# The additions and subtractions of five rotations, on GpSimd and not on VectorE

## The chip, the core and the metric

The kernel runs on one core of a Trainium2 chip. The metric is the device time of one execution in microseconds, as the median of repeated runs. The core has five engines with a queue each: TensorE (PE) for matrix products and transposes, VectorE (DVE), ScalarE (ACT) and GpSimd (POOL) for elementwise work, and SyncE (SP), which here only issues DMAs. GpSimd issues some DMAs too. Each engine takes its instructions in the order in which they stand in its queue.

## What is computed

Two transformer layers on x of 4 x 512 x 512 floats. Layer 0 is an attention of 32 heads of 16 with one shared key and value, and a linear layer with dequantised weights. Layer 1 is an attention of 32 query heads of 128 over 8 key and value heads, with rotary position embedding, and a feed-forward part with ternary octonion weights. Cut to the part that matters here:

```python
def _rotate_half(x):
    x1, x2 = (x[..., :HEAD_DIM // 2], x[..., HEAD_DIM // 2:])
    return jnp.concatenate([-x2, x1], axis=-1)
...
q = (hidden_states @ Wq.T).reshape(bsz, q_len, N_HEADS, HEAD_DIM).transpose(0, 2, 1, 3)
...
q = q * cos + _rotate_half(q) * sin
k = k * cos + _rotate_half(k) * sin
...
scores = jnp.einsum('bhqd,bhkd->bhqk', q, k) * scale
...
x = x + _layernorm(_L1_attn_ref(_layernorm(x, axis=-1), ...), axis=-1)
```

## The kernel before

**Numbers.** Matrix products run on a rounded float type (F32R). To keep accuracy a value is split into a high part (a cast) and a low part (value minus high part), and a product becomes three: high by high, high by low, low by high (`mm3`, lines 183 to 185; `mm3_gen`, lines 160 to 162). A 128 x 512 product over 512 is so 12 matmuls.

**Stages.** First comes layer 0 for the four batches (class `A1`, with the tail of each 128-row tile in `A2.post`: output projection, layer norms, linear layer, layer 1's first norm, and the values of layer 1, products with the weights called `wv`). `post` takes tiles through `add_norm`, whose norm has a power on GpSimd (L108), and adds a shift to a tile on GpSimd (L813) before it is stored for the last stage. Then `phase_b` does layer 1's attention, and class `C` the feed-forward part.

**Units.** `phase_b` works in 32 units, u = 0 to 31: unit u is key head g = u // 4 of batch b = u % 4, with the four query heads of that group. For each unit there is one `kproj` (the rotated key) and four `qproj` (the rotated queries q0 to q3), 12 matmuls each. In a unit's 16 steps, `score` makes one 128-row block of scores of one query head: matmuls into a PSUM bank of `ps` (L960 and L961 for the first block, with a mask addition L962 on VectorE; L965 to L967 for the others), a fused mask and row minimum on VectorE (L969), the exponential on ScalarE (L973), a reciprocal (L975) and a scaling on GpSimd (L976). `trans` transposes four of these (L985) and splits them (L988, L989), `pv` multiplies by the values (L998 to L1000) and `oproj` projects into the accumulator. The projections of unit u + 1 stand among the steps of unit u. Unit 0's projections have no unit before them: they stand where layer 0's last tiles end. This stretch, from some 640 to 700 us, is called the passage below.

**Rotation.** `rope` (lines 845 to 854) takes a projection in PSUM and makes both parts of the rotated tile: three products on VectorE (L848, L850, L851), an addition (L852) on the engine `eng`, a cast on ScalarE (L853), and a subtraction (L854) on `eng`. Its scratch tiles `rp_a` and `rp_b` come from a pool with one buffer each, so a rotation can start only when the one before has read `rp_a` for the last time, at L854. A PSUM bank of a projection is free after L851.

**Banks.** Unit 0's projections use the three `ps` banks that the scores use too (`proj_bank`); later ones use the two `mm` banks, shared with `oproj` and the last tiles of layer 0.

**Weights.** `load_w` loads a head's weight twice: as F32R by a DMA from GpSimd's queue (L888, `w_h`), and as it is by a DMA from SP's queue (L890, `raw`, one buffer), and subtracts on GpSimd (L891, `w_l`). SP also issues the copies of `Tern.expand` (L1145) and the loads of the input tiles (L898, L899).

**Order.** The program is recorded in the order of the Python code, and a scheduler then sets the order of the instructions in every queue from its own model of when each could run. A change of one instruction's engine can so move others, in every queue.

Of the kernel before, what the change touches and what calls it, by code (L numbers as in the profile page):

```python
# [42 lines left out]
def f(ap):  # L43
    return ap.bitcast(F32)
# [134 lines left out]
def mm3(nc, ps, lh, ll, rh, rl, ks):  # L179

    n = len(ks)
    for j, k in enumerate(ks):
        nc.tensor.matmul(ps, lh(k), rh(k), start=(j == 0), stop=False)  # L183
        nc.tensor.matmul(ps, lh(k), rl(k), start=False, stop=False)  # L184
        nc.tensor.matmul(ps, ll(k), rh(k), start=False, stop=(j == n - 1))  # L185
# [659 lines left out]
def rope(nc, tmp, dst_h, dst_l, ps, cos, sin, eng):  # L845

    a = tmp.tile([128, S], F32, name="rp_a", tag="rp_a")
    nc.vector.tensor_tensor(a, ps, cos, ALU.mult)  # L848
    r = tmp.tile([128, S], F32, name="rp_b", tag="rp_b")
    nc.vector.tensor_tensor(r[0:64], ps[64:128], sin[0:64], ALU.mult)  # L850
    nc.vector.tensor_tensor(r[64:128], ps[0:64], sin[64:128], ALU.mult)  # L851
    eng.tensor_tensor(a, a, r, ALU.add)  # L852
    nc.scalar.copy(dst_h, a)  # L853
    eng.tensor_tensor(dst_l, a, f(dst_h), ALU.subtract)  # L854


def phase_b(tc, nc, c, aps, xt_d, wk_d, v_d, acc, xp, P, tern, tail):

    if True:
        tmp = P(name="bt", bufs=1)  # L860
# [59 lines left out]
        def proj_bank(u):  # L920

            if u == 0:
                return psS.tile([128, S], F32, name="ps", tag="ps")
            return mmp.tile([128, S], F32, name="mm", tag="mm")

        def kproj(u):
            wh, wl = W["k", u // 4]
            xh, xl = X[u]
            ps = proj_bank(u)
            mm3(nc, ps, lambda k: wh[:, bass.ts(k, 128)], lambda k: wl[:, bass.ts(k, 128)],  # L930
                lambda k: xh[:, k], lambda k: xl[:, k], range(KC))
            k = kvp.tile([128, 2, S], F32R, name="k", tag="k")
            rope(nc, tmp, k[:, 0], k[:, 1], ps, cosk, sink, nc.vector if u < 1 else nc.gpsimd)
            K[u] = k

        def qproj(u, j):
            h = 4 * (u // 4) + j
            wh, wl = W["q", h]
            xh, xl = X[u]
            ps = proj_bank(u)  # L940
            mm3(nc, ps, lambda k: wh[:, bass.ts(k, 128)], lambda k: wl[:, bass.ts(k, 128)],
                lambda k: xh[:, k], lambda k: xl[:, k], range(KC))
            qh = qp.tile([128, S], F32R, name="qh", tag="qh")
            ql = qp.tile([128, S], F32R, name="ql", tag="ql")
            rope(nc, tmp, qh, ql, ps, cosq, sinq, nc.vector if u < 1 else nc.gpsimd)
            Q[u, j] = qh, ql

        PS = {}
# [76 lines left out]
        cosk, sink, cosq, sinq = (cp.tile([128, S], F32, name=n) for n in ("cosk", "sink", "cosq", "sinq"))  # L1025
# [4 lines left out]
        for j in range(4):  # L1030
            wh, wl = (wqp.tile([128, 512], F32R, name="w_" + e, tag="w_" + e) for e in "hl")
            split(nc, wh, wl, first[:, j], nc.gpsimd)
            W["q", j] = wh, wl
        kproj(0)
        for j in range(4):
            qproj(0, j)
# [7 lines left out]
        for p in range(NU * 16 + 12):  # L1044
            G, j = p // 4, p % 4
            u, qb = G // 4, G % 4
# [16 lines left out]
            if j == 1 and u + 1 < NU:  # L1063
                qproj(u + 1, qb)
                if (u + 1) % 4 == 3 and u // 4 < 7:
                    load_w("q", u // 4 + 1, qb)
            if j == 3 and qb == 0 and u + 1 < NU:
                kproj(u + 1)
                if (u + 1) % 4 == 3 and u // 4 < 7:
                    load_wk(u // 4 + 1)  # L1070
# [333 lines left out]
```

## Time and profile before

| | us |
|---|---|
| median of 3 runs (2329.95 to 2330.2) | 2330.18 |
| the profiled execution's own time | 2329.53 |
| span of the profiled execution, first to last instruction | 2327.8 |
| TensorE busy | 2276.1 |
| VectorE busy | 1578.9 |
| ScalarE busy | 1069.9 |
| GpSimd busy | 1174.8 |

In the profile's lines, `out<-in` are tile names, L numbers are lines of the kernel, `x` is a count, and `[t <-E tile L]` is the idle time of the engine before the instruction and what ended it. The waits view lists who waited for whom: total us, times, longest. "PEclk" is the share of TensorE's full clock that was granted. The time of the execution is 1.7 us more than its span.

### The profile page before, as it was taken

The numbers are of one execution on the slowest core, as the hardware profiler recorded it, in microseconds if no ns is written. First come the engines' busy times: TensorE is split into PE (matmuls) and PEld (weight loads), VectorE is DVE, ScalarE is ACT, GpSimd is POOL, SyncE is SP. The second block draws the span as 40 slices with busy tenths as digits, with TensorE's granted clock in tenths as the row PEclk, the third lists the DMA queues.
The fourth block names the chain that finished last, engine by engine and source line by source line (L and its number), as shares of the span: only waits on it lengthen the run. The fifth ranks groups of instructions, "written<-read, shape, count | busy, mean of one in ns | idle before, by whom it ended". The sixth has DMA issues, their size and how long they took to land.

```text
span 2327.8 us, 35950 instructions
## 1 busy us (share of the span) xinstructions
PE 2276.1 (98%) x11638; PEld 1789.9 (77%) x11638; DVE 1578.9 (68%) x4662; ACT 1069.9 (46%) x2408; POOL 1174.8 (50%) x1388
## 2 busy tenths in 40 slices
PE   7999999999989999999999999999999999999998
PEld 5666566666678888888888888888888888878886
DVE  6766767685477777777777777777777778764443
ACT  6655545454334444444444444444444445543332
POOL 3323443434246665765665765765665767522211
PEclk9999999999999999999999999999999999999999
DMA  3655463525362413413313313323322312051000
GB/s 92 200 156 176 116 164 74 160 82 163 123 212 82 127 66 98 125 66 101 122 66 104 119 66 106 117 66 109 113 67 106 98 63 78 10 158 37 32 23 19
DMA packets 155535, 236.31 MB, mean 102 GB/s; under 512 B 26274, under 2 KB 91042, under 8 KB 146516
## 3 DMA queue, kind: packets, MB, share of 16 engines
q1 hardware_dynamic: 137732, 195.33, 26.9%
q0 software_dynamic: 14768, 35.92, 5.4%
q10 hardware_dynamic: 2848, 2.76, 0.4%
q8 instruction: 93, 1.52, 0.3%
q14 instruction: 94, 0.77, 0.1%
HBM read 180.03 MB, written 61.83 MB: 104 GB/s over the span
## 4 chain that ended last, share of the span: by engine, by line
PE 87%; issue 4%; DMA 4%; DVE 2%; ACT 2%; POOL 1%; SPq 0%; ACTq 0%; POOLq 0%; DVEq 0%
PE mm L183 11%; PE mm L184 11%; PE mm L185 11%; PE pt L985 6%; PE mm L160 3%; PE mm L161 3%; PE mm L162 3%; PE po L998 3%; PE po L999 3%; PE po L512 3%; PE po L1000 3%; PE ps L965 3%; PE ps L966 3%; PE ps L967 3%; PE gu L1218 3%
## 5 line engine op out<-in xcount | busy, mean ns | idle before, releaser
L976 POOL TENSOR_TENSOR s<-s,r 128x384 f32<-128x384 f32 (+3 forms) x512 | 359.0, 720 | 117.5 <-DVE r L975 106.8
L973 ACT ACTIVATE s<-s,mn 128x384 f32<-128x384 f32 (+3 forms) x512 | 286.1, 560 | 239.8 <-DVE mn L969 230.6
L852 POOL TENSOR_TENSOR rp_a<-rp_a,rp_b 128x512 f32<-128x512 f32 x155 | 200.2, 1292 | 279.8 <-DVE rp_b L851 266.7
L988 ACT CAST ph<-pt 128x512 fp32r<-128x512 f32 x320 | 181.4, 586 | 289.9 <-PE pt L985 287.6
L461 DVE CUSTOM_DVE_ANT_0 jk<-ps,mask 128x384 bf16<-128x384 f32 (+3 forms) x512 | 228.8, 482 | 73.1 <-PE ps L457 72.0
L989 DVE TENSOR_TENSOR pl<-pt,ph 128x512 fp32r<-128x512 f32 x320 | 216.3, 687 | 39.8 <-ACT ph L988 36.6
L969 DVE CUSTOM_DVE_ANT_0 s<-ps,mask 128x384 f32<-128x384 f32 (+2 forms) x384 | 203.2, 552 | 39.2 <-PE ps L967 18.9
L499 ACT ACTIVATE pe<-pt 128x512 f32<-128x512 f32 x307 | 175.1, 601 | 90.8 <-PE pt L496 82.2
L985 PE MATMUL pt<-ident,s 128*128 128x128 f32 x1280 | 211.8, 272 | 0.2 <-DVE pl L989 0.2
L183 PE MATMUL mm<-w_h,oh 128*128 128x512 f32 x512 | 203.7, 398 | 0.9 <-ACT oh L1004 0.9
L184 PE MATMUL mm<-w_l,oh 128*128 128x512 f32 x512 | 201.9, 394 | 0.5 <-POOL w_l L891 0.5
L185 PE MATMUL mm<-w_h,ol 128*128 128x512 f32 x512 | 200.4, 391 | 0.0
L985 PEld LDWEIGHTS pt<-ident,s 128*128 128x128 f32 x1280 | 164.3, 140 | 45.4 <-DVE pl L989 0.4
L183 PE MATMUL mm<-xh,w_h 128*128 128x512 f32 x496 | 198.8, 401 | 0.0
L185 PE MATMUL mm<-xh,w_l 128*128 128x512 f32 x496 | 197.0, 397 | 0.0
L501 POOL TENSOR_SCALAR_AFFINE_SELECT pe<-pe 128x512 f32<-128x512 f32 x128 | 83.4, 655 | 224.4 <-ACT pe L499 219.4
L184 PE MATMUL mm<-xl,w_h 128*128 128x512 f32 x496 | 195.8, 395 | 0.0
L854 POOL TENSOR_TENSOR ql<-rp_a,qh 128x512 fp32r<-128x512 f32 x124 | 160.3, 1293 | 47.4 <-ACT qh L853 46.3
L848 DVE TENSOR_TENSOR rp_a<-mm,cosq 128x512 f32<-128x512 f32 x124 | 85.6, 690 | 120.2 <-PE mm L185 89.7
L1004 ACT CAST oh<-po 128x512 fp32r<-128x512 f32 x128 | 74.4, 582 | 152.8 <-PE po L1000 152.4
L965 PE MATMUL ps<-k,qh 128*128 128x384 f32 (+2 forms) x384 | 141.2, 368 | 1.0 <-DVE mn L969 0.9
L108 POOL TENSOR_TENSOR ln_rs<-ln_ve,mhalf 128x1 f32<-128x1 f32 x112 | 63.7, 576 | 152.8 <-DVE ln_ve L106 139.0
(349 smaller groups left out, 5853.4 us busy)
## 6 DMA issues: line engine op xcount, KB each, us to landing
xh<-xt SPq DMA_DIRECT2D x32, 1024.0 KB
xl<-xt SPq DMA_DIRECT2D x32, 1024.0 KB
raw<-in_a_wo SPq DMA_DIRECT2D x32, 256.0 KB
vh<-v SPq DMA_DIRECT2D x32, 256.0 KB
vl<-v SPq DMA_DIRECT2D x32, 256.0 KB
w_h<-in_a_wo POOLq DMA_DIRECT2D x32, 256.0 KB, 3.3
m_d<-t_d SPq DMA_DIRECT2D x192, 42.5 KB
raw<-in_a_wq SPq DMA_DIRECT2D x28, 256.0 KB
```

What stands on the lines that cost most here:

```text
L183: nc.tensor.matmul(ps, lh(k), rh(k), start=(j == 0), stop=False)
L184: nc.tensor.matmul(ps, lh(k), rl(k), start=False, stop=False)
L185: nc.tensor.matmul(ps, ll(k), rh(k), start=False, stop=(j == n - 1))
L461: nc.vector.tensor_tensor_reduce(out=jk[:, :nk], in0=p, in1=self.c.mask[:, 384 - 128 * qb:512], scale=-1.0, scalar=3e38, op0=ALU.add, op1= ...
L852: eng.tensor_tensor(a, a, r, ALU.add)
L965: nc.tensor.matmul(ps[:, :nk], qh[:, qs], k[:, 0, :nk], start=True, stop=False)
L969: nc.vector.tensor_tensor_reduce(out=s[:, :nk], in0=ps[:, :nk], in1=mask, scale=-1.0, scalar=3e38, op0=ALU.add, op1=ALU.min, accum_out=mn)
L973: nc.scalar.activation(s[:, :nk], s[:, :nk], AF.Exp, bias=mn, scale=-1.0, accum_out=l)
L976: nc.gpsimd.tensor_tensor(s[:, :nk], s[:, :nk], r.to_broadcast([128, nk]), ALU.mult)
L985: nc.tensor.transpose(pt[:, j], PS[u, qb, j][:, bass.ts(kb, 128)], c.ident)
L988: nc.scalar.copy(ph, pt)
L989: nc.vector.tensor_tensor(pl, pt, f(ph), ALU.subtract)
```

## The change

`kproj` and `qproj` hand `rope` the engine for its addition and its subtraction. Before, this was VectorE for unit 0 and GpSimd for the 31 others; after, it is GpSimd for all.

```diff
-            rope(nc, tmp, k[:, 0], k[:, 1], ps, cosk, sink, nc.vector if u < 1 else nc.gpsimd)
+            rope(nc, tmp, k[:, 0], k[:, 1], ps, cosk, sink, nc.gpsimd)
...
-            rope(nc, tmp, qh, ql, ps, cosq, sinq, nc.vector if u < 1 else nc.gpsimd)
+            rope(nc, tmp, qh, ql, ps, cosq, sinq, nc.gpsimd)
```

Five rotations of unit 0 are concerned (one key, four queries), with two instructions each.

## The prediction

> **What bounds the kernel now.** I read the page's first part, then the busy time by stage, then TensorE's waits inside the stage of the change and after it, then the timeline there.
>
> ```profile
> PE 2276.1 (98%) x11638; PEld 1789.9 (77%) x11638; DVE 1578.9 (68%) x4662; ACT 1069.9 (46%) x2408; POOL 1174.8 (50%) x1388
> ```
>
> TensorE is busy 98% of the span, so a change counts only where it opens or closes one of TensorE's gaps. The next view cuts the span into attention of layer 0, the passage to layer 1 (unit 0's rotations lie here), the other units, and the rest; columns are length, PE, PEld, DVE, ACT, POOL busy, TensorE's clock, DMA.
>
> ```profile
> 0.00:640.00 640.00, 607.40 (x3338) 406.61 (x3338) 422.07 (x1586) 336.50 (x622) 237.00 (x356) 0.99 0.48 137
> 640.00:700.00 60.00, 53.62 (x238) 43.34 (x239) 45.47 (x110) 22.43 (x51) 29.20 (x37) 0.94 0.65 206
> 700.00:2030.00 1330.00, 1328.62 (x6772) 1110.18 (x6771) 968.53 (x2630) 606.76 (x1562) 841.13 (x918) 1.00 0.28 91
> 2030.00:2328.00 298.00, 286.44 (x1294) 229.72 (x1292) 142.86 (x337) 104.23 (x174) 67.42 (x79) 0.99 0.18 53
> ```
>
> From 700 to 2030 TensorE lacks 1.4 us of 1330: there is nothing to win. In the 60 us of the passage it lacks 6.4 us, and its clock is 0.94. TensorE's waits in that window:
>
> ```profile
> PE ps L960 <- DVE mn L969: 2.7, 1, 2.7
> PE ps L183 <- DVE rp_b L851: 2.1, 1, 2.1
> PE ps L965 <- DVE mn L969: 0.9, 2, 0.4
> PE mm L160 <- ACT ph L150: 0.7, 1, 0.7
> ```
>
> The second ends with the first rotation's last product (L851), which the change does not touch. The first is the one in reach: the fourth score of unit 0 needs a `ps` bank that the first L969 frees. Why is L969 late? VectorE's timeline, with TensorE's score below:
>
> ```profile
> 675.12 0.69 DVE L848 TENSOR_TENSOR rp_a<-mm,cosk 128x512 f32<-128x512 f32 x1 [1.21 <-POOL ql L854]
> ...
> 680.70 0.69 DVE L848 TENSOR_TENSOR rp_a<-mm,cosq 128x512 f32<-128x512 f32 x1 [1.20 <-POOL k L854]
> ...
> 686.28 0.69 DVE L848 TENSOR_TENSOR rp_a<-mm,cosq 128x512 f32<-128x512 f32 x1 [2.76 <-POOL ql L854]
> ...
> 689.01 0.28 DVE L969 CUSTOM_DVE_ANT_0 s<-ps,s 128x128 f32<-128x128 f32 x1
> ...
> 689.36 0.57 PE L960 MATMUL ps<-k,qh 128*128 128x256 f32 x1 [2.72 <-DVE mn L969]
> ```
>
> L969 stands in VectorE's queue behind the rotations. `rp_a` has one buffer, so rotations form one chain, and each L848 waits for the subtraction (L854) of the one before. Nine rotations begin before L969: five of unit 0 and four of unit 1.
>
> **The cost of an operation.** From the instructions on `rp_a`:
>
> ```profile
> L852 POOL TENSOR_TENSOR rp_a<-rp_a,rp_b x155: 1265/1292/1316, 671.0 to 2018.0; 128x512 f32<-128x512 f32 x155
> L854 POOL TENSOR_TENSOR ql<-rp_a,qh x124: 1274/1294/1308, 673.8 to 2020.7; 128x512 fp32r<-128x512 f32 x124
> L852 DVE TENSOR_TENSOR rp_a<-rp_a,rp_b x5: 682/684/691, 643.4 to 666.0; 128x512 f32<-128x512 f32 x5
> L854 DVE TENSOR_TENSOR ql<-rp_a,qh x4: 683/692/750, 653.4 to 667.4; 128x512 fp32r<-128x512 f32 x4
> ```
>
> Ten instructions leave VectorE (10 x 0.69 = 6.9 us) and come to GpSimd (10 x 1.29 = 12.9 us). One rotation's turn is 680.70 - 675.12 = 5.58 us on GpSimd; on VectorE the shortest is 663.90 - 659.47 = 4.43 us (L848 to L848). So the chain's bare price is 5 x 1.15 = 5.75 us. [...]
>
> **The order moves too.** The scheduler writes another order for all engines from the middle of the passage. Up to the fourth score TensorE gets the same amount of work in both programs (kproj and three qproj of unit 1 included); what differs is that only eight rotations, not nine, begin before the first L969, and L969 is put after the eighth's second product. One turn less is 5.58 us, which nearly pays the 5.75. So I follow the new order with the trace's durations (matmul of 512 columns 0.233 us apart, L848 to L851's end 2.10, handover to GpSimd 0.14, add 1.28, cast 0.62 with 0.04 and 0.07 beside it, subtraction 1.29, 0.04 back).
>
> k starts at 639.91 as before; its products end at 642.0, so TensorE's 2.1-us wait stays. Add 642.14, cast, subtraction to 645.44. The rotation of q0 starts at 645.5 (before: 648.22, as it stood behind the split of a transposed tile). TensorE does q3's projection at 648.2, ahead of most of the wv products. On GpSimd q0's add stands behind L813 (1.57) and three L108 (0.53 each): 648.6; its subtraction behind two more L813: 653.3 to 654.6. That delay is covered: q1's L848 stands in VectorE's queue behind two splits whose transposes TensorE reaches at 654.0 to 655.0, so q1 starts at 656.45. Then one L813 in its turn: q2 starts at 662.9. q3 stands behind the mask addition (L962) of the second score, which TensorE reaches at 669.05, behind wv products and kproj: 669.75 (GpSimd was done at 669.0). From here the chain runs free at 5.58: q(1,0) 675.3, k(1) 680.9, q(1,1) 686.5. Two products later, at 687.9, comes L969, 0.29 long: the fourth score starts at 688.2 instead of 689.36, **1.15 us earlier**. All along TensorE has matmuls: qproj(1,1) is reached at 678.0 with its bank free at 677.4, qproj(1,2) at 683.6 with its bank free at 683.0. Work ends at 686.4, so the wait shrinks from 2.7 to about 1.8 us.
>
> What else queues behind the moved instructions: the last tiles' L108 comes up to 5.6 us later (649.04 to about 654.6), but its transposes are not reached before 665.6. L813's x2 stores go out a little later on SP's queue and are read only in the last stage; VectorE's 6.9 us are returned beside an idle queue and bring nothing by themselves.
>
> After the scores: on GpSimd the six DMA issues of `w_h` (L888, 689.72 to 693.05, so 3.33 us) follow k(1)'s subtraction at 686.45, then q(1,1)'s add, one L891 and four L976 (0.36 each): 693.9, when unit 0's first transposes start; before it was 694.21. q(1,1)'s subtraction comes behind four longer L976, at 696.1 to 697.4, and holds q(1,2)'s L848 until 697.8 and so the bank of qproj(1,3) until 699.9; before, qproj(1,3) started at 701.24. That lead of 1.2 agrees with the first. At 717.34 TensorE waited 0.46 us for the fourth `w_l` (L891); its raw load is now issued before the eight L1145 copies and not behind them, and I count 0.15 of it as gained.
>
> From there TensorE is full. Whether it stays so is the one thing no row shows. I counted, in the two orders, for each TensorE wait on another engine, how much matmul work lies between its last TensorE ancestor and itself: under 1.5 us in 24 of 1836 waits before, in 9 of 1869 after; under 2.5 us in 92 and 51. The cover is no thinner, so I keep the 1.4 us lost there, with +-1 us.
>
> **The clock.** The rows first:
>
> ```profile
> 686.00:690.00 4.00, 1.28 (x6) 0.84 (x5) 3.53 (x11) 1.25 (x4) 1.73 (x3) 0.93 0.22 66
> 690.00:693.00 3.00, 3.00 (x16) 3.00 (x15) 2.65 (x16) 2.69 (x12) 3.00 (x6) 0.53 0.81 246
> ```
>
> After the 2.7-us wait TensorE runs at half clock to 692.8, about 3.4 us, which can cost 1.7. A wait of 1.8 us may or may not bring it (one of 2.14 did, one of 1.2 at 574.6 did not). I count nothing for it, since with the slow clock the first transposes still wait for GpSimd at 693.9. [...]
>
> **Sum.** -1.15 - 0.15 = -1.3 us on the profiled execution's 2329.53 (span 2327.8 and 1.7 around it), which lies 0.65 below the median; on the median, 2330.18 - 1.3 = 2328.9. This is within the 0.2% (4.7 us) that a measurement of this kernel can tell from no change. Own range, by 1 us on the walk and 1 us on the later units: 2327.0 to 2330.9.
>
> **Rivals.** *Slower: the chain is exposed.* If the order saves no turn, because L969 in fact waits for a ninth subtraction or q1 and q3 start late (GpSimd's L813 once took 2.08 instead of 1.57), the five turns fall on the wait before L960: 5.75 us, 2335.9. It decides once L969 starts after about 693.7 (4.7 us late). Against it: TensorE sets q1's and q3's starts with 0.8 us and more to spare. For it: only 0.6 us spare at the two bank releases. Chance 0.20, with any new wait that recurs by unit counted in (0.15 us in each of 31 would do), since the new order of 1330 us is the part that no row shows.
> *Faster: the gap goes altogether.* 2.7 us, the half clock's 1.7 and the later 0.9 of waits for L969: -5.3, 2324.9. It needs L969 by 686.4, 1.5 us before my walk. Chance 0.10.
> *Nothing: gained and given back.* GpSimd's queue (six issues, L891 waiting for its raw load) holds q(1,2) longer than I count, and the lead of 1.2 is spent on qproj(1,3)'s bank: 2330.2 to 2332. Chance 0.14. The change does what it says, since the order shows ten more such instructions on GpSimd and ten fewer on VectorE.
>
> **How the numbers follow.** My forecast has 0.56. Within 0.2% are it and the third rival, 0.70; faster 0.10; slower 0.20. The range reaches down to 1 us below the walk's lower bound and up to the slower rival's bare price, 2326.0 to 2336.0; the faster case and the half of the slower one that lies above its price are the 2 in 10 left out.
>
> **What would show it.** In the profile after: L852 and L854 x160 on GpSimd and none on VectorE; q0's L848 near 645.5, q1's near 656.5, q(1,1)'s near 686.5; the L960 wait near 1.8 us, the score at 688.2; the stage 700 to 2030 still within 2 us of full. A rotation start over 1 us off, or TensorE waits above 3 us after 700, would make the prediction wrong.

## The result, and the profile after

The change makes the kernel slower: 2334.69 us (median of 13 runs, 2331.82 to 2341.28) against 2329.95 us in the runs beside it, a ratio of 1.003 with a 95% interval of 1.0022 to 1.0038. That is 4.7 us more, where the prediction said 1.3 less. The measured time lies in the predicted range; the sign was missed. The profiled execution took 2336.24 us with a span of 2334.5.

The engines' busy times, and the columns of the busy time by stage as before (length, PE, PEld, DVE, ACT, POOL, TensorE's clock, DMA):

```profile
PE 2278.3 (98%) x11638; PEld 1790.6 (77%) x11638; DVE 1568.9 (67%) x4652; ACT 1074.4 (46%) x2408; POOL 1188.3 (51%) x1398
```

```profile
640.00:700.00 60.00, 53.61 (x241) 43.07 (x239) 39.17 (x100) 22.00 (x50) 40.85 (x48) 0.94 0.66 206
700.00:2030.00 1330.00, 1326.09 (x6744) 1106.22 (x6743) 961.68 (x2624) 609.40 (x1557) 841.40 (x915) 1.00 0.28 91
```

The edit itself is as foreseen: ten instructions fewer on VectorE, ten more on GpSimd. The passage looks as before (53.61 us of TensorE in 60 against 53.62). The other units don't: TensorE got through 6744 instructions in these 1330 us and not 6772. Its waits from 700 to 2030 us, in the changed kernel:

```profile
PE mm L183 <- DVE rp_b L851: 3.2, 5, 1.2
PE po L998 <- DVE ol L1005: 0.3, 1, 0.3
PE ps L965 <- DVE mn L969: 0.2, 1, 0.2
```

Before, the same view is

```profile
PE mm L184 <- POOL w_l L891: 0.5, 1, 0.5
PE po L998 <- DVE ol L1005: 0.3, 1, 0.3
PE mm L183 <- ACT oh L1004: 0.3, 1, 0.3
PE pt L985 <- DVE pl L989: 0.2, 1, 0.2
```

The first line of the changed kernel is new: before has no wait of a projection (L183) for a rotation's last product (L851) in this stretch. The rotations that it waits for are those of the later units, which the change doesn't touch.

**The stages by work.** TensorE runs the same 11,638 instructions in every kernel here. So I cut each trace at the starts of the 3250th, the 3750th and the 10,500th of them (counted from 0), and took the differences of these times; before, the cuts lie at 620, 734 and 2059 us. The first 3356 have the same order in before and after, so what differs in the first part is scatter between executions.

| us | start to 3250th | to 3750th (passage) | to 10,500th (later units) | to the last |
|---|---|---|---|---|
| before | 612.27 | 114.20 | 1324.45 | 259.37 |
| after | 613.35 | 113.97 | 1329.21 | 260.67 |
| after, second profile (e9) | 614.71 | 115.00 | 1329.16 | 260.67 |

The passage changed by -0.23 and +0.80 us; the later units by +4.76 and +4.71; the end by +1.30 in both. In the later units the loss grows step by step, one step every 175 us, which is four units. This is where most of the time went.

**What happens there.** The largest step, in the changed kernel's timeline of GpSimd, VectorE and TensorE (brackets: idle time before, and what ended it):

```profile
1855.10 1.28 POOL L891 TENSOR_TENSOR w_l<-raw,w_h 128x512 fp32r<-128x512 f32 x1 [1.77 <-DMA w_h<-in_a_wq]
...
1859.41 1.28 POOL L891 TENSOR_TENSOR w_l<-raw,w_h 128x512 fp32r<-128x512 f32 x1 [3.03 <-DMA raw<-in_a_wo]
1860.65 1.29 POOL L852 TENSOR_TENSOR rp_a<-rp_a,rp_b 128x512 f32<-128x512 f32 x1
...
1863.42 1.29 POOL L891 TENSOR_TENSOR w_l<-raw,w_h 128x512 fp32r<-128x512 f32 x1 [1.12 <-DMA raw<-in_a_wo]
1864.66 1.30 POOL L854 TENSOR_TENSOR ql<-rp_a,qh 128x512 fp32r<-128x512 f32 x1
...
1866.00 0.69 DVE L848 TENSOR_TENSOR rp_a<-mm,cosk 128x512 f32<-128x512 f32 x1 [1.81 <-POOL ql L854]
...
1868.15 0.50 PE L183 MATMUL mm<-xh,w_h 128*128 128x512 f32 x1 [1.20 <-DVE rp_b L851]
```

Read it from the bottom. TensorE waits for an `mm` bank that is free after L851; that rotation's L848 waited for the last reader of `rp_a`, L854 of the rotation before; and L854 stood in GpSimd's queue behind an L891 that was waiting for its `raw` load. `raw` has one buffer, so each load starts only when the L891 before it is through, and three L891 in a row come 4.3 and 4.0 us apart.

The two programs differ here in the order of GpSimd's queue. With W for L891, A for L852, S and K for L854 of a query and a key, and a dot for each L976:

```
before (order B)   W A W . S W A . . K
after  (order A)   W W A . W S . A K
```

Either order comes back in every fourth unit. In order A the second W stands ahead of the A, in order B behind it. The orders of the other queues differ between A and B too; A and B name the whole order of the later units.

### The profile page after: what moved, and what is told of

Same layout as the page of the kernel before. It is cut to its first block, busy times and chain, and to the rows that moved or that the text cites. A ratio compares the mean times of both kernels' runs of the same rounds, so it can differ in the third digit from the quotient of the medians.

```text
span 2334.5 us, 35949 instructions
## 1 busy us (share of the span) xinstructions
PE 2278.3 (98%) x11638; PEld 1790.6 (77%) x11638; DVE 1568.9 (67%) x4652; ACT 1074.4 (46%) x2408; POOL 1188.3 (51%) x1398
## 4 chain that ended last, share of the span: by engine, by line
PE 85%; DMA 5%; issue 4%; DVE 3%; ACT 2%; POOL 2%; SPq 0%; ACTq 0%; POOLq 0%; DVEq 0%
PE mm L183 11%; PE mm L184 10%; PE mm L185 10%; PE pt L985 5%; PE mm L160 3%; PE po L512 3%; PE mm L161 3%; PE mm L162 3%; PE po L999 3%; PE po L1000 3%; PE po L998 3%; PE ps L965 3%; PE ps L966 3%; PE ps L967 3%; PE gu L1218 3%
## 5 line engine op out<-in xcount | busy, mean ns | idle before, releaser
L976 POOL TENSOR_TENSOR s<-s,r 128x384 f32<-128x384 f32 (+3 forms) x512 | 360.7, 722 | 113.5 <-DVE r L975 106.0
L852 POOL TENSOR_TENSOR rp_a<-rp_a,rp_b 128x512 f32<-128x512 f32 x160 | 207.3, 1296 | 305.3 <-DVE rp_b L851 300.2
L969 DVE CUSTOM_DVE_ANT_0 s<-ps,mask 128x384 f32<-128x384 f32 (+2 forms) x384 | 204.6, 552 | 38.1 <-PE ps L967 18.4
L183 PE MATMUL mm<-w_h,oh 128*128 128x512 f32 x512 | 203.6, 398 | 1.3 <-ACT oh L1004 0.7
L183 PE MATMUL mm<-xh,w_h 128*128 128x512 f32 x496 | 199.2, 402 | 2.8 <-DVE rp_b L851 2.6
L854 POOL TENSOR_TENSOR ql<-rp_a,qh 128x512 fp32r<-128x512 f32 x128 | 165.6, 1294 | 17.7 <-ACT qh L853 17.7
L848 DVE TENSOR_TENSOR rp_a<-mm,cosq 128x512 f32<-128x512 f32 x124 | 85.6, 690 | 98.4 <-PE mm L185 88.9
L965 PE MATMUL ps<-k,qh 128*128 128x384 f32 (+2 forms) x384 | 140.2, 365 | 0.9 <-DVE mn L969 0.8
L975 DVE RECIPROCAL r<-l 128x1 f32<-128x1 f32 x512 | 74.7, 158 | 92.8 <-ACT s L973 90.7
```

The costliest lines, as they stand in the source:

```text
L965: nc.tensor.matmul(ps[:, :nk], qh[:, qs], k[:, 0, :nk], start=True, stop=False)
L969: nc.vector.tensor_tensor_reduce(out=s[:, :nk], in0=ps[:, :nk], in1=mask, scale=-1.0, scalar=3e38, op0=ALU.add, op1=ALU.min, accum_out=mn)
L976: nc.gpsimd.tensor_tensor(s[:, :nk], s[:, :nk], r.to_broadcast([128, nk]), ALU.mult)
```

## The experiments

Two theories. **The order:** the loss is order A, which the scheduler happens to write once unit 0's instructions have moved; unit 0's own instructions cost nothing. **The moved work:** ten instructions at nearly twice the time (L852 1.296 us on GpSimd in after, 0.684 on VectorE in before) cost what they cost, in proportion, wherever the wait shows. The scheduler's orders, as built, allow them to be told apart: of the 32 ways to put unit 0's five rotations on the two engines, 13 give order A (q0 alone is one of them) and 19 order B (all but q0 is one). Four of the 32 were run.

**e1, q0 alone; e2, all but q0.** The edit, with 2 and 29 in place of MASK (bit 0 stands for k, bits 1 to 4 for q0 to q3):

```diff
-rope(nc, tmp, k[:, 0], k[:, 1], ps, cosk, sink, nc.gpsimd)
+rope(nc, tmp, k[:, 0], k[:, 1], ps, cosk, sink, nc.vector if u < 1 and not MASK & 1 else nc.gpsimd)
...
-rope(nc, tmp, qh, ql, ps, cosq, sinq, nc.gpsimd)
+rope(nc, tmp, qh, ql, ps, cosq, sinq, nc.vector if u < 1 and not MASK >> j + 1 & 1 else nc.gpsimd)
```

> Of the five rotations of layer 1's first unit only q0's addition and subtraction are on GpSimd (2 of the change's 10 instructions); in GpSimd's queue the later units stand in the changed kernel's order (two subtractions for w_l ahead of an addition once in four units). Theory of the order (the loss is a recurring wait in the later units: GpSimd waits for a raw load at L891 with a rotation behind it): nearly the whole loss, 3 to 6 us over before, and TensorE's excess over its nominal pitch from 720 to 2040 us near 7 us with waits at L183 for L851. Theory of the moved work (each rotation moved costs its share): a fifth, about 1 us over before, and an excess near 2.5.

> The other four rotations of the first unit (k, q1, q2, q3; 8 of the 10 instructions) are on GpSimd and q0's stays on VectorE; the later units stand in the order of the kernel before. Theory of the order: no loss, -1.5 to +0.5 us against before, excess from 720 to 2040 us near 1.5. Theory of the moved work: four fifths of the loss, about 3.8 us over before, excess near 6.

| | median us | ratio to before (95%) | passage | later units | end |
|---|---|---|---|---|---|
| e1 | 2329.73 | 1.000 (0.999 to 1.001) | 110.01 | 1328.03 | 260.96 |
| e2 | 2330.95 | 1.0007 (0.9997 to 1.0016) | 114.73 | 1323.78 | 260.96 |

The later units follow the theory of the order: +3.6 us over before with two instructions moved, -0.7 with eight. But e1's time is against the theory of the order: it isn't 3 to 6 us over before, since its passage is 4.2 us shorter. The 1 us over before of the other theory lies inside its interval (2.3 us either way), so e1's time alone would not speak against that one; e2's 3.8 us over lies just outside. e2, 0.8 us over before, is 0.3 above the theory of the order, within its interval. The shorter passage comes again in e8 and e11 and is looked at below.

**e3 and e4, no second load.** After and before, with L891 waiting for no `raw`:

```diff
-raws = P(name="braw", bufs=1)
...
-raw = raws.tile([128, 512], F32, name="raw", tag="raw")
-nc.sync.dma_start(raw, src)
-nc.gpsimd.tensor_tensor(wl, raw, f(wh), ALU.subtract)
+nc.gpsimd.tensor_tensor(wl, f(wh), f(wh), ALU.subtract)
```

> The changed kernel without the raw loads of layer 1's later weights: w_l = w_h - w_h, so the subtraction L891 stays on GpSimd but waits for no second load (the low parts of these weights are zero, which leaves that part of the computation out). Theory of the order and the load: the excess from 720 to 2040 us falls from 6.9 to 2 or less, and the time is within 1 us of the next run's, 2328 to 2331. Theory of the moved work: the loss stays, 4 to 5 us over the next run.

> The same edit in the kernel before (no raw loads of the later weights, low parts zero), as the partner of the run above. Both theories: within 1.5 us of before, since TensorE lost only 1.5 us from 720 to 2040 there and 0.5 of it to a w_l.

Medians 2328.48 (ratio 0.9994, 0.9985 to 1.0002) and 2329.67 (0.9998, 0.9988 to 1.0008), 1.2 us apart where 1 was expected at most; later units 1322.39 and 1322.68 us. Without the loads the two engines' placements differ by 0.3 us in the later units and not by 4.8. The scheduler writes a third order for these two programs, so this pair takes away the loads and order A together and can't divide the loss between them. (Both profiled executions had 10.2 us of half clock in the passage, which took 115.83 and 116.11 us, so only the later units are compared.)

**e5, e6 and e7, the same work in the other order.** The first four w_o loads are written in reverse, which turns the later units of after into order B, those of before into order A, and those of e1 into order B:

```diff
 for j in range(4):
-    load_w("o", 0, j)
+    load_w("o", 0, 3 - j)
```

> The changed kernel, all ten instructions on GpSimd, with the first four w_o loads written in the order 3, 2, 1, 0; the same work, but GpSimd's queue in the later units then stands in the order of the kernel before. Theory of the order: no drift from 735 to 2060 us (0 +-1.5 against before, where the changed kernel had +4.8), no TensorE wait for L851 above 0.3 us there, and a time of 2329 to 2332. Theory of the moved work: the drift and the time of the changed kernel, about 2334.7.

> The kernel before, nothing moved to GpSimd, with the same reversed writing; its later units then stand in the order of the changed kernel. Theory of the order: a drift of +3 to +5 us from 735 to 2060 us with TensorE waits at L183 for L851 in every fourth unit, and a time of 2332.5 to 2336. Theory of the moved work: none, 2330 +-1.

> Only q0's rotation on GpSimd and the reversed writing: the passage of e1, which was 4.2 us shorter than before, with the later units in the order of the kernel before. Theory of the order: 2325 to 2327.5, faster than both kernels. Theory of the moved work: as e1, 2329.7.

| | order | median us | ratio to before (95%) | passage | later units | end |
|---|---|---|---|---|---|---|
| e5 | B | 2333.34 | 1.0020 (1.0010 to 1.0030) | 114.84 | 1323.71 | 261.57 |
| e6 | A | 2338.90 | 1.0042 (1.0030 to 1.0054) | 115.44 | 1329.66 | 260.93 |
| e7 | B | 2327.07 | 0.9991 (0.9980 to 1.0002) | 114.33 | 1323.69 | 259.38 |

e6 decides between the theories: nothing is moved to GpSimd, and the later units lose 5.2 us, 0.2 more than expected, with the changed kernel's wait. (Its GpSimd order is A in six of the seven places where the loads come back.) From 735 to 2040 us in e6:

```profile
PE mm L183 <- DVE rp_b L851: 2.1, 4, 1.0
PE po L998 <- DVE ol L1005: 0.3, 1, 0.3
```

The totals were less tidy. e5 and e6 came out 1.3 and 2.9 us above what the theory of the order allowed. A part of this is a price of the reversed writing: the first output projection needs the load that now comes last (`w_l` L891 holds TensorE for 1.4 us in e6 where before has 0.5), and the passage and the end of e6 are together 2.8 us longer than before's. e7's passage is 4.3 us longer than e1's, 1.7 of it by half clock after its first wait. e7's time lies inside its range, but its interval reaches to 1.0002, so it can't be told from before. For e5 the parts after the 3250th instruction add up to 2.1 us over before, just under its interval (1.0010 to 1.0030 is 2.3 to 7.0 us); I leave the rest open.

**e8, a second buffer for raw.** e1 with

```diff
-raws = P(name="braw", bufs=1)
-sp = P(name="bs", bufs=8)
+raws = P(name="braw", bufs=2)
+sp = P(name="bs", bufs=7)
```

> Only q0's rotation on GpSimd, and a second buffer for raw (paid for with one of the eight buffers of the scores, s), so that a raw load no longer waits for the subtraction before it; the whole computation. Theory of the order and the load: GpSimd's waits for raw fall from 18.7 us (735 to 2040 us) below 8, no TensorE wait for L851 recurs, and the time is 2325 to 2328, unless the seven buffers of s bring a wait of their own (then TensorE waits at L985 or L960). Theory of the moved work: as e1, 2329.7.

It took 2353.66 us (ratio 1.0103, 1.0090 to 1.0116). GpSimd's waits for `raw` fell to 4.7 us as expected, but the scheduler wrote yet another order, and in that one 28 us are lost in the later units (1352.31). From 735 to 2040 us:

```profile
PE mm L183 <- DVE rp_b L851: 3.3, 9, 0.7
PE po L999 <- DVE pl L989: 1.2, 3, 0.6
```

These two lines are 4.5 us of the 28; where the rest goes was not followed. The load wait is so not the only thing that can hold a rotation, and both theories missed this time. What the new order costs and what the seven buffers of `s` cost was not separated.

**e9 to e11, the smallest edit.** e9 is the changed kernel again. e10 is the changed kernel with `for j in (0, 1, 3, 2)` for the first w_o loads, which gives order B and leaves the first load first; e11 is e1 with `(0, 2, 1, 3)`, also order B.

> The changed kernel once more, unchanged, as the partner of the next run on the same chip, and as a second profile of its stages. Both theories: about 4 to 5 us over before; the drift from 735 to 2060 us again near +4.8.

> The changed kernel with only the last two of the first four w_o loads swapped (order 0, 1, 3, 2), the smallest edit found that puts the later units into the order of the kernel before. Theory of the order: drift -0.7 +-0.7 from 735 to 2060 us, no TensorE wait for L851 above 0.3 us there, and a time 3 to 6 us under the run above. Theory of the moved work: as the run above. If the drift goes but the time stays within 1.5 us of the run above, the loss lies in the passage or at the end, not in the later units.

> Only q0's rotation on GpSimd, w_o loads in the order 0, 2, 1, 3; the later units stand in the order of the kernel before, and the passage should lose less at the first output projection than with the reversed writing (e7: 2.8 us over e1 there). Theory of the order: drift -0.7 +-0.7 and 2 to 5 us under before. Theory of the moved work: 0 to 1 us over before.

| | order | median us | ratio to before (95%) | passage | later units | end |
|---|---|---|---|---|---|---|
| e9 | A | 2335.30 | 1.0024 (1.0010 to 1.0037) | 115.00 | 1329.16 | 260.67 |
| e10 | B | 2327.98 | 0.9995 (0.9984 to 1.0006) | 114.43 | 1323.68 | 259.37 |
| e11 | B | 2324.54 | 0.9978 (0.9969 to 0.9987) | 110.07 | 1323.88 | 260.56 |

With all ten instructions on GpSimd and two loads swapped, e10 is 7.3 us under e9 on the same chip, 1.3 more than the upper end expected. The parts after the 3250th instruction add up to it: 1704.83 - 1697.48 = 7.35, of which 5.5 in the later units, 1.3 at the end and 0.6 in the passage. e11 is 5.0 us under the runs of before beside it (2329.53), at the edge of what was expected. Ten slower instructions cost nothing that can be told from zero (0.9995, 0.9984 to 1.0006); the loss comes with the order that they bring about.

The later units sort by the order and not by the moved work. In the six programs with order B (0, 2, 8 or 10 instructions moved) they take 1323.68 to 1324.45 us; within these six TensorE, VectorE, ScalarE and GpSimd each have the same order in the later units. In the four executions with order A (three programs; 0, 2 or 10 moved) they take 1328.03 to 1329.66. That shows the order as a whole to be the cause; which queue in it does the harm is read from the traces. e10's waits from 735 to 2040 us, and the stretch that answers to the one shown of after:

```profile
PE po L998 <- DVE ol L1005: 0.3, 1, 0.3
PE pt L985 <- DVE pl L989: 0.2, 1, 0.2
```

```profile
1849.64 1.30 POOL L891 TENSOR_TENSOR w_l<-raw,w_h 128x512 fp32r<-128x512 f32 x1 [0.88 <-DMA w_h<-in_a_wq]
...
1852.17 1.31 POOL L852 TENSOR_TENSOR rp_a<-rp_a,rp_b 128x512 f32<-128x512 f32 x1 [1.24 <-DVE rp_b L851]
...
1853.64 1.29 POOL L891 TENSOR_TENSOR w_l<-raw,w_h 128x512 fp32r<-128x512 f32 x1 [0.16 <-DMA raw<-in_a_wo]
...
1855.24 1.29 POOL L854 TENSOR_TENSOR ql<-rp_a,qh 128x512 fp32r<-128x512 f32 x1
...
1856.57 0.69 DVE L848 TENSOR_TENSOR rp_a<-mm,cosk 128x512 f32<-128x512 f32 x1 [1.17 <-POOL ql L854]
...
1857.72 1.29 POOL L891 TENSOR_TENSOR w_l<-raw,w_h 128x512 fp32r<-128x512 f32 x1 [1.19 <-DMA raw<-in_a_wo]
```

L852 and L854 run while the loads are under way: after the first L891 it takes 6.9 us to the key's L848 (1856.57 - 1849.64), in after 10.9 (1866.00 - 1855.10).

**How the 5.5 us divide.** I compared the spacing of TensorE's starts in after with the usual spacing of the same instructions. What exceeds it falls into two kinds. The first is the chain shown above, in every fourth unit: 0.80, 0.85, 0.02, 0.54, 0.30 and 1.47 us, together 4.0. Its size changes from step to step with the load, and its length doesn't: in after, e1, e6 and e9 I found 17 such waits, and in all of them TensorE starts 4.71 to 4.74 us after the third L891. So in these the moment at which `raw` lands sets TensorE's start. No run took away the load's wait and kept order A, so the part of the load rests on this reading. The second kind is 0.28 us, six times, together 1.7 (4.0 and 1.7 are 0.2 more than the 5.5), at an output projection whose `mm` bank an L851 holds. In after's timeline of VectorE the rotation stands behind L1005, which waits for ScalarE:

```profile
882.32 0.69 DVE L1005 TENSOR_TENSOR ol<-po,oh 128x512 fp32r<-128x512 f32 x1 [2.99 <-ACT oh L1004]
882.92 0.68 DVE L848 TENSOR_TENSOR rp_a<-mm,cosq 128x512 f32<-128x512 f32 x1
```

In e10 that L848 stands ahead of L1005. At the end `PE mm L148 <- DVE xn L167` holds TensorE for 0.9 us in after and in e9 and isn't there in before and e10, which accounts for most of the end's 1.3 us. It doesn't go with A and B, though: e11, in order B and without this wait, takes 260.56 us at the end. What sets the end's length stays open.

## Why the prediction was wrong

**The bound: right.** TensorE's gaps and its clock were what counted, and VectorE's 10 us less of work (1578.9 to 1568.9) didn't make the kernel faster.

**The walk through the passage: right in its order, and in its times partly by luck.** Eight rotations begin before the first L969, and the fourth score waits less:

```profile
687.00 0.69 DVE L848 TENSOR_TENSOR rp_a<-mm,cosq 128x512 f32<-128x512 f32 x1 [1.77 <-POOL k L854]
...
688.44 0.29 DVE L969 CUSTOM_DVE_ANT_0 s<-ps,s 128x128 f32<-128x128 f32 x1
...
688.89 0.35 PE L960 MATMUL ps<-k,qh 128*128 128x256 f32 x1 [2.21 <-DVE mn L969]
```

This execution was 0.88 us late at the 3250th instruction. With that taken off, the eight rotations start within 0.75 us of the walk and the score at 688.01, where 688.2 was predicted. One turn on GpSimd took 5.58 us as in the sum (687.00 - 681.42). The 0.46-us wait for `w_l` at 717 us is gone, where 0.15 of it was counted. But the walk took over before's clock, which fell to half at the first wait (641.62 us, for 3.41 us). In this execution that stretch didn't come, and in e9 it came twice as long (6.83 us). There, counted in the same way, the rotations from q1 on start 1.2 to 1.6 us later than the walk, and the score comes at 689.95, 0.6 later than in before. So the 1.15 us that were forecast are less than what the clock at the first wait shifts from one execution to the next.

**The clock: a step that was mis-sized.** I counted nothing for half clock. After the score, the changed kernel's clock is

```profile
690.00:693.00 3.00, 2.34 (x10) 2.29 (x10) 2.39 (x18) 2.25 (x10) 2.99 (x4) 0.50 1.07 290
693.00:697.00 4.00, 3.98 (x15) 3.48 (x14) 1.70 (x9) 1.88 (x6) 4.00 (x9) 0.53 0.35 114
```

6.83 us of half clock, twice what before had at this place (3.41). Taking half of TensorE's busy time at half clock as lost (an estimate from the granted 0.50), the passage loses 3.1 us by it in after, 3.2 in before (1.5 of it at the first wait, where after has none), and nothing in e1 and e11, where the L960 wait is 1.1 us. So what after was ahead at the score is lost again behind it, and over the whole passage the clock takes the same in both.

The idle time is the same too, 7.13 us in after and 7.19 in before. What the waits for L969 (L960 and L965) and for `w_l` gave back, about 1.2 us, went to two waits for L851 that before doesn't have. From 640 to 735 us in after:

```profile
PE ps L183 <- DVE rp_b L851: 2.8, 2, 2.1
PE ps L960 <- DVE mn L969: 2.2, 1, 2.2
...
PE mm L183 <- DVE rp_b L851: 0.6, 1, 0.6
```

The first line holds the known 2.1 us and 0.6 at 648.5 us; the last is an output projection at 712 us, held by the rotation of unit 1's q3, which starts at 709.88 us where before had it at 704.30. That is why the passage as a whole gained only 0.23 us or lost 0.80, and not the 1.3 of the sum. The third rival, gained and given back, had the kind of this right.

The absent half clock is also most of e1's 4.2. (By the same count e1 also idles 1.8 us less; the two together are 0.8 more than the 4.2, about the error of such a count.) Of the price per turn only one of five is paid there, and the order has eight rotations ahead of L969 too. The prediction's faster rival came near this size, -5.3 us to 2324.9; e11 measured 2324.54, with one rotation moved and not five. Its sum was another: the L960 wait did not go, and 1.5 us of the clock's part lie at the first wait, where half clock also stayed away in after.

**The later units: the step that failed.** "The cover is no thinner, so I keep the 1.4 us lost there, with +-1 us." It was 4.8 us longer than before. The count behind it went, as the prediction words it, by TensorE waits on another engine and the matmul work since the last TensorE ancestor. A DMA's landing has no place in it, so an L891 that waits for `raw` looked like an L891 that is ready, and L852 and L854 behind it looked covered. The third rival named this mechanism, L891 waiting for its load and holding rotations, but only in the passage; the slower rival named the size (0.15 us in each of 31 units would do; 4.8 over 31 is 0.154) but with another mechanism and only a part of its 0.20. What was missed is that `load_w` comes back in every fourth unit. The second kind of loss, 1.7 of the 5.7 us, has no load in it; why the count passed over it stays open. The prediction's own alarm, TensorE waits above 3 us after 700, is what the profile after shows.

The price of the moved work (L852 took 1.296 us on GpSimd in after, 0.684 on VectorE in before) is not where the loss is: e10 pays it for the same five rotations and is level with before, and e6 pays none and is the slowest of these but e8.

## What to carry to other kernels

Where a scheduler writes the order, an edit in one corner can give another order to a periodic part that it never touched; compare the orders of the whole program, and follow every wait in them back through the DMA landings as well as the engines. Look first for instructions that wait for a load with a single buffer, and for what stands behind them in their queue. To test such a loss, find a neutral edit that turns the order with the work unchanged; here two swapped loads were worth 7.3 us, more than the engines of ten instructions.

## What the runs showed of the chip

In the passage the clock fell to half with waits of 2.1 us and more, and not each time. The same wait, 2.1 us of TensorE for the first L851, came with half clock in before and e7 (some 3.4 us of it) and in e9 (6.83), and with none in after, e1, e2, e8, e10 and e11.

In before the clock stood at 0.50 for 3.41 us each from 34.04, 494.84, 552.87, 641.62 and 689.40 us on; in after for 3.41 us each from 34.57, 44.81, 495.37 and 553.40 us on and for 6.83 from 689.93. In both it stood at 0.50 again from 2320.97 and 2328.33 us to the end, when TensorE had no more work. Why the same wait comes with half clock in one execution and not in another was not shown.

A fall of 3.41 us costs up to 1.7 us (half of it, an estimate for a TensorE that has work; in before matmuls of 512 columns came 0.43 us apart at half clock, from 642.64 us, and 0.23 at full clock, from 636.75), and a single execution of one kernel scatters by such falls and by the first loads (TensorE's first 200 instructions took 59.3 to 64.5 us): before ranged from 2324.16 to 2336.32 us in 35 runs, and the stretch up to the 3250th instruction, the same for TensorE in before, after and nine of the experiments, took 610.35 to 617.97 us. So a change of 0.2% shows only in the medians of many executions and in the stages by work.
